# Batch-normalised pair products on one core: the head rebuilt, and the short rows' products moved

## The chip, the cores and the metric

One core of a Trainium2 chip runs the whole kernel. The metric is the device time of one execution in microseconds; the kernel before takes 1979.55 us (median of three runs, 1979.31 to 1979.63). The core has TensorE (PE, its weight loads shown as PEld), VectorE (DVE), ScalarE (ACT), GpSimd (POOL), and SyncE (SP), which here issues DMA transfers only. A q behind an engine's name (ACTq, SPq) stands for its instructions that issue transfers. PSUM is the memory that TensorE writes its results to, SBUF the working memory.

## The reference

All numbers are float32. `r_xi` and `r_xj` have shape 1024 x 39 x 16. For each pair of a row r and a smaller column c (741 pairs, the lower triangle of 39 x 39), the 16 x 16 outer product of a batch entry is normalised over the batch and its own 256 elements, scaled and shifted by the pair's gamma and beta, and multiplied by one 16 x 16 matrix W. The output is 1024 x 1 x 741 x 16 x 16, 777 MB.

```python
cross = xj[:, rows, :, None] * xi[:, cols, None, :]
mean = jnp.mean(cross, axis=(0, 2, 3), keepdims=True)
var = jnp.mean(jnp.square(cross - mean), axis=(0, 2, 3), keepdims=True)
normed = (cross - mean) * jax.lax.rsqrt(var + BN_EPS)
normed = normed * gamma[None, :, None, None] + beta[None, :, None, None]
out = normed[:, :, None, :, :] * W[None, None, :, :, :]
```

## The kernel before, in words

**Layout.** The batch is laid out as 128 partitions x 8 entries (`t`). The whole of xi and xj stays in SBUF. With the scale s and the shift t of a pair, an output element is (s xi xj + t) W.

**The head** (L66 to L240) finds s and t. The x arrays come in four pieces each, xj through SP's queue and xi through ACT's. Gamma and beta come as 38 one-row transfers each, gamma through SP (L83), beta through ACT (L84), into 39 x 39 squares. The first two batch entries give a shift for each field (row sums on VectorE, L109; a matmul of ones, L115; the shift written by ScalarE, L126). Then for each of four pieces and both arrays a deviation from the shift is made (L135, five on POOL and three on VectorE, three buffers), squared on ScalarE (L142), summed on VectorE (L144), and the mean's deviation is put beside it (L146). Gram matmuls (L158) sum over the batch. ScalarE copies the three results (L178), a chain of 39 x 39 operations on VectorE makes the variance and the reciprocal root (L191 to L215). To bring s and t of each pair to all partitions, VectorE spreads six rows at a time with a diagonal `eye` (L221), a matmul of ones copies them to 128 partitions (L228), and ScalarE copies each row out of PSUM into `st_sb` (L236).

**The body** makes the output in tiles of one row r and two batch entries; each row has four tiles, t0 = 0, 2, 4, 6. The order of tiles (L247 to L256) starts with row 19 and then pairs each long row r with the short row 38 - r: 20 with 18, 21 with 17, up to 37 with 1, and at last 38 alone. A long tile and its short partner together have 38 columns and fill one half of the buffer `y_sb`; the next two batch entries use the other half. For a tile, `scale_xi` (L267, POOL) multiplies xi by s into one of two `xs` buffers. `products` multiplies xs by each of the 16 elements of xj, for both batch entries: 24 operations on ScalarE (L292) and 8 on POOL (L294), each writing every 16th element of the tile, so that each waits until the stores of the old contents of the tile's whole place have landed. Where r is 6 or less (`VECTOR_ROW`), VectorE makes the products in two broadcast operations instead (L282). `finish` adds t and multiplies by W, one operation a column on VectorE (L319); for rows above 6, 13% of the columns are done by POOL (L305 and L309). It stores the tile in pieces of at most 14 columns through SP (L327), the POOL columns in the last piece.

**Order.** Each engine works through its instructions in program order. The code is written out by hand as a software pipeline (L332 on): in step k the products of tile k+1, the scaling for tile k+2, then the finishing of tile k; a short tile's products, made by VectorE, come behind the finishing of the tile ahead of it.

## Time and profile before

| what | value |
|---|---|
| median of three runs | 1979.55 us (1979.31 to 1979.63) |
| the profiled execution | 1979.6 us, span 1977.9 us |
| busy: DVE, ACT, POOL, PE | 1802.4, 1519.2, 1437.4, 18.6 us |
| written to HBM | 776.99 MB, 395 GB/s over the span |
| first store issued | 92.6 us |

The span reaches from the first to the last instruction; 1.7 us of the execution lie around it. The slices of the page cut the span into 40 equal parts of 49.4 us. Their digits are busy tenths, and the line DMA is the mean busy share of 16 DMA engines. In a table of stretches the DMA share reads 1.01 where the transfers have no gap.

### The profile page before, as it was taken

To read this page: it belongs to the slowest core of one execution; us is meant where nothing else is said; L and a number is where in the kernel's file an instruction comes from. 1 tells how busy PE (TensorE), PEld (TensorE's weight loads), DVE (VectorE), ACT (ScalarE), POOL (GpSimd) and SP (SyncE) were. 2 spreads that over 40 slices of the span, in tenths; PEclk is the share of its full clock that TensorE was granted. 3 is DMA by queue.
4 is the path that set the end of the run, shared out by engine and by line. 5 is a ranking of instruction groups with operands and counts; after the bars stand their busy time and mean duration, and the time that the engine had idled before them with its cause. 6 is when DMAs were issued, how large, how long until landed. Compare 5 with 4: busy or idle time off the path is not lost. (4 is left out here: it accounts for less than half of the span.)

```text
span 1977.9 us, 9219 instructions
## 1 busy us (share of the span) xinstructions
PE 18.6 (1%) x70; PEld 11.8 (1%) x70; DVE 1802.4 (91%) x2694; ACT 1519.2 (77%) x3127; POOL 1437.4 (73%) x1693
## 2 busy tenths in 40 slices
...
DMA  2199999999999999999999999999999999999998
GB/s 106 47 421 421 420 421 421 421 421 421 422 425 425 423 425 425 425 423 425 424 421 422 420 421 418 412 389 386 393 392 403 403 411 411 407 407 403 395 379 375
DMA packets 79760, 782.84 MB, mean 396 GB/s; under 512 B 4905, under 2 KB 5929, under 8 KB 14153
## 3 DMA queue, kind: packets, MB, share of 16 engines
...
q10 hardware_dynamic: 652, 2.56, 0.3%
...
q14 instruction: 72, 0.58, 0.1%
HBM read 5.25 MB, written 776.99 MB: 395 GB/s over the span
## 5 line engine op out<-in xcount | busy, mean ns | idle before, releaser
L319 DVE SCALAR_TENSOR_TENSOR y_sb<-y_sb,st_sb,w_dve 128x512 f32<-128x512 f32 x2588 | 1711.0, 742 | 133.5 <-issue 96.7
L292 ACT ACTIVATE y_sb<-xs,xj_sb 128x320 f32<-128x320 f32 (+21 forms) x3072 | 1500.8, 581 | 366.2 <-DMA out_dram<-y_sb 324.6
L294 POOL TENSOR_SCALAR y_sb<-xs,xj_sb 128x320 f32<-128x320 f32 (+22 forms) x1024 | 556.7, 566 | 188.9 <-DMA out_dram<-y_sb 155.3
L309 POOL TENSOR_TENSOR y_sb<-y_sb,w_sb 128x1024 f32<-128x1024 f32 (+4 forms) x128 | 431.2, 3369 | 10.7
L267 POOL TENSOR_TENSOR xs<-xi_sb,st_sb 128x608 f32<-128x608 f32 (+37 forms) x152 | 190.0, 1253 | 275.5 <-DVE y_sb L282 178.5
L305 POOL TENSOR_SCALAR y_sb<-y_sb,st_sb 128x512 f32<-128x512 f32 x376 | 253.8, 692 | 1.7 <-ACT y_sb L292 1.7
L282 DVE TENSOR_TENSOR y_sb<-xs,xj_sb 128x1536 f32<-128x1536 f32 (+5 forms) x48 | 50.1, 1085 | 0.0
L135 POOL TENSOR_TENSOR dev<-xj_sb,shift 128x1248 f32<-128x1248 f32 x4 | 9.3, 2325 | 36.4 <-ACT shift_r L129 28.8
L126 ACT ACT_TABLE_LOAD x1 | 1.3, 1283 | 29.8 <-DMA b_sq<-in_L_rec_beta_dram 29.8
L142 ACT ACTIVATE dev<-dev 128x1248 f32<-128x1248 f32 x8 | 9.9, 1243 | 14.7 <-POOL dev L135 11.5
L146 DVE SCALAR_TENSOR_TENSOR fa<-total,shift 128x78 f32<-128x78 f32 x4 | 3.1, 764 | 11.1 <-ACT shift_r L129 11.1
L109 DVE TENSOR_REDUCE total<-xj_sb 128x78 f32<-128x1248 f32 x4 | 5.8, 1454 | 8.0 <-DMA xj_sb<-in_r_xj_dram 8.0
L236 ACT COPY st_sb<-ps 128x38 f32<-128x38 f32 (+37 forms) x38 | 4.3, 219 | 8.7 <-PE ps L228 8.7
L228 PE MATMUL ps<-wide,ones 39*128 39x468 f32 (+1 forms) x14 | 10.2, 921 | 5.7 <-DVE wide L221 5.7
L221 DVE TENSOR_TENSOR wide<-stq,eye 39x468 f32<-39x468 f32 (+1 forms) x7 | 4.0, 593 | 3.7 <-PE ps L228 3.6
L144 DVE TENSOR_REDUCE fb<-dev 128x78 f32<-128x1248 f32 x4 | 5.7, 1442 | 1.4 <-ACT dev L142 1.4
L144 DVE TENSOR_REDUCE fa<-dev 128x78 f32<-128x1248 f32 x4 | 5.8, 1444 | 1.0 <-ACT dev L142 1.0
L158 PE MATMUL ps_g<-fb,fa 128*39 128x79 f32 x32 | 5.8, 338 | 41.4 <-DVE fb L144 41.4
L109 DVE TENSOR_REDUCE total<-xi_sb 128x78 f32<-128x1248 f32 x4 | 5.8, 1443 | 0.0
L135 DVE TENSOR_TENSOR dev<-xi_sb,shift 128x1248 f32<-128x1248 f32 x3 | 5.2, 1773 | 0.0
L146 DVE SCALAR_TENSOR_TENSOR fb<-total,shift 128x78 f32<-128x78 f32 x4 | 5.2, 1290 | 0.0
L158 PEld LDWEIGHTS ps_g<-fb,fa 128*39 128x39 f32 x32 | 4.3, 182 | 42.0 <-issue 30.9
...
## 6 DMA issues: line engine op xcount, KB each, us to landing
...
```

What stands on the lines that cost most here:

```text
L109: nc.vector.tensor_reduce(total[:, t0 : t0 + TS, x], src[:, t0 : t0 + TS], AX.X, ALU.add)
L135: engine.tensor_tensor(dev, src[:, t0 : t0 + TS], shift[:, x : x + 1, :].unsqueeze(3).to_broadcast([P, TS, F, E]), ALU.subtract,)
L144: nc.vector.tensor_reduce(to, dev, AX.X, ALU.add)
L158: nc.tensor.matmul(acc[0:F, 0 : 2 * F + 1], lhs, fb[:, t], start=t == 0, stop=t == NT - 1)
L228: nc.tensor.matmul(ps.rearrange("p r x f -> p (r x f)"), ones[0:F, :], wide.rearrange("p r f -> p (r f)"), start=True, stop=True,)
L267: nc.gpsimd.tensor_tensor(xs, xi_sb[:, t0 : t0 + T, 0:r, :], s_sb[:, :, n0 : n0 + r, :].to_broadcast([P, T, r, E]), ALU.mult,)
L282: nc.vector.tensor_tensor(y[:, t], xs[:, t].unsqueeze(2).to_broadcast([P, r, E, E]), xj_sb[:, t0 + t, r : r + 1, :].unsqueeze(3).to_broadc ...
L292: nc.scalar.activation(y[:, t, :, i, :], xs[:, t], AF.Copy, scale=scale)
L294: nc.gpsimd.tensor_scalar(y[:, t, :, i, :], xs[:, t], scale, 1.0, ALU.mult, ALU.mult)
L305: nc.gpsimd.tensor_scalar(y[:, :, c, :], y[:, :, c, :], t_sb[:, n0 + c : n0 + c + 1], 1.0, ALU.add, ALU.mult)
L309: nc.gpsimd.tensor_tensor(y[:, :, split:r, :], y[:, :, split:r, :], w_sb.unsqueeze(1).to_broadcast([P, T, r - split, EE]), ALU.mult,)
L319: nc.vector.scalar_tensor_tensor(y[:, :, c, :], y[:, :, c, :], t_sb[:, n0 + c : n0 + c + 1], w_dve.to_broadcast([P, T, EE]), ALU.add, ALU. ...
```

## The change

1. Gamma and beta are loaded by one broadcast each to all partitions (`gb_all`), beta still through ACT's queue. The 39 x 39 chain ends in the bare reciprocal root and in minus mean times root; gamma and beta are applied behind the spreading.
2. Rows are spread by one small matmul for each row, with a selector `pick[:, r, :]` (39 x 128, ones in partition r) as weights; POOL makes all 39 selectors in one operation on 4992 elements in a partition. Two VectorE operations a group bring the result through gamma and beta into `st_sb`. The first group is row 19 alone.
3. The four tiles of row 19 take the four quarters of `y_sb`. Scratch of the head lies in the third and fourth quarter: seven deviation buffers, and everything else with the selectors.
4. The products of the first two tiles are made from xi without s ("raw"), on ScalarE between the statistics' steps, and the last 12 of the second tile on POOL. When s and t are known, `affine` applies them in place, even columns on ScalarE, odd ones on POOL, and `weigh` multiplies by W on VectorE, several columns in one operation. The first tile is stored in pieces of 3, 6 and 10 columns.
5. All eight deviations are made by POOL. The fa/fb step reads the shift from PSUM (`ps_u`). The copy of W into PSUM is made early.
6. `VECTOR_ROW` is gone: rows 1 to 6 have their products made by ScalarE and POOL as all others, and rows 4 to 6 give POOL one column.

```diff
 BN_EPS = 1e-5
-VECTOR_ROW = 6
 PIECE = 14
+FIRST_PIECES = (0, 3, 9, 19)
-DEV_ON_VECTOR = ((2, 1), (4, 1), (6, 1))
-ROW_GROUPS = ((19, 25), (13, 19), (25, 31), (7, 13), (31, 37), (1, 7), (37, 39))
+ROW_GROUPS = ((19, 20), (15, 19), (20, 25), (25, 32), (1, 15), (32, 39))
...
-    ) as devp, tc.tile_pool(name="ps", bufs=1, space=bass.MemoryType.PSUM) as psp, tc.tile_pool(
...
-        for r in range(1, F):
-            n0 = first[r]
-            nc.sync.dma_start(g_sq[r : r + 1, 0:r], gamma[n0 : n0 + r].unsqueeze(0))
-            nc.scalar.dma_start(b_sq[r : r + 1, 0:r], beta[n0 : n0 + r].unsqueeze(0))
...
-        for r0, r1 in ROW_GROUPS:
-            n = r1 - r0
-            wide = devp.tile([F, n, 2 * F], F32, tag="wide", name="wide")
-            nc.vector.tensor_tensor(
-                wide,
-                stq.rearrange("p x f -> p (x f)").unsqueeze(1).to_broadcast([F, n, 2 * F]),
-                eye[:, r0:r1].unsqueeze(2).to_broadcast([F, n, 2 * F]),
-                ALU.mult,
-            )
...
-            for r in range(r0, r1):
-                nc.scalar.copy(st_sb[:, :, first[r] : first[r] + r], ps[:, r - r0, :, 0:r])
...
+    flat = y_sb.rearrange("p n e -> p (n e)")
+    place = {"dev": half * EE, "rest": (half + half // 2) * EE}
+    stop = {"dev": (half + half // 2) * EE, "rest": 2 * half * EE}
...
+    devs = [scratch("dev", P, T, F, E) for _ in range(7)]
+    ones = scratch("rest", P, P)
+    pick = scratch("rest", F, F, P)
+    gb_all = scratch("rest", P, 2, NP)
...
+    def raw_products(n, engine, steps):
+        r, t0, _ = tiles[n]
+        for step in steps:
+            t, i = divmod(step, E)
+            yield lambda t=t, i=i: product(n, engine, t, i, xi_sb[:, t0 + t, 0:r, :])
+    def emit(work, count):
+        for _, step in zip(range(count), work):
+            step()
...
-            if r <= VECTOR_ROW:
-                nc.vector.tensor_tensor(
-                    y[:, t],
-                    xs[:, t].unsqueeze(2).to_broadcast([P, r, E, E]),
-                    xj_sb[:, t0 + t, r : r + 1, :].unsqueeze(3).to_broadcast([P, r, E, E]),
-                    ALU.mult,
+            for i in range(E):
+                product(n, nc.scalar if i < E - POOL_I else nc.gpsimd, t, i, xs[:, t])
...
+    def affine(n):
+        r = tiles[n][0]
+        y = view(n)
+        for c in range(r):
+            s_c = st_sb[:, 0, first[r] + c : first[r] + c + 1]
+            t_c = t_sb[:, first[r] + c : first[r] + c + 1]
+            if c % 2 == 0:
+                nc.scalar.activation(y[:, :, c, :], y[:, :, c, :], AF.Identity, bias=t_c, scale=s_c)
+            else:
+                nc.gpsimd.tensor_scalar(
+                    y[:, :, c, :], y[:, :, c, :], s_c, t_c, ALU.mult, ALU.add
                 )
...
+    def weigh(n, bounds):
+        y = view(n)
+        for c0, c1 in zip(bounds, bounds[1:]):
+            nc.vector.tensor_tensor(
+                y[:, :, c0:c1, :],
+                y[:, :, c0:c1, :],
+                w_dve.unsqueeze(1).to_broadcast([P, T, c1 - c0, EE]),
+                ALU.mult,
+            )
+            store(n, c0, c1)
...
-        split = r - (int(r * POOL_SHARE + 0.5) if r > VECTOR_ROW else 0)
+        y = view(n)
+        split = r - int(r * POOL_SHARE + 0.5)
...
-        for k in range(len(tiles)):
-            if k + 1 < len(tiles) and tiles[k + 1][0] > VECTOR_ROW:
-                products(k + 1)
-            if k + 2 < len(tiles):
-                scale_xi(k + 2)
-            finish(k)
-            if k + 1 in xs_of:
-                products(k + 1)
+        nc.gpsimd.dma_start(w_sb[:, 0, :], w.rearrange("o i j -> (o i j)").partition_broadcast(P))
+        nc.sync.dma_start(gb_all[:, 0], gamma.partition_broadcast(P))
+        nc.scalar.dma_start(gb_all[:, 1], beta.partition_broadcast(P))
+        nc.gpsimd.memset(ones, 1.0)
+        nc.gpsimd.affine_select(
+            out=pick, in_=ones[0:F, :].unsqueeze(1).to_broadcast([F, F, P]),
+            compare_op=ALU.is_equal, fill=0.0, base=0,
+            pattern=[[-1, F], [0, P]], channel_multiplier=1,
+        )
...
+        def deviation(n):
+            t0, x = n // 2 * T, n % 2
+            nc.gpsimd.tensor_tensor(
+                devs[n % 7],
+                sources[x][:, t0 : t0 + T],
+                shift[:, x : x + 1, :].unsqueeze(3).to_broadcast([P, T, F, E]),
+                ALU.subtract,
+            )
...
+            stt(
+                to[:, t0 : t0 + T, 0:F],
+                total[:, t0 : t0 + T, part(x)],
+                1.0 / E,
+                ps_u[:, x : x + 1, :].to_broadcast([P, T, F]),
+                ALU.mult,
+                ALU.subtract,
+            )
...
+        raw0 = raw_products(0, nc.scalar, range(32))
+        raw1 = raw_products(1, nc.scalar, range(20))
+        sums(0)
+        emit(raw0, 8)
+        nc.scalar.copy(w_dve, w_sb)
...
+        ps_u = ps_s[:, 2 * F : 4 * F].rearrange("p (x f) -> p x f", x=2)
+        nc.scalar.copy(ps_u, shift)
+        sums(2)
+        for n in range(7):
+            deviation(n)
+        for n in range(2 * NT // T):
+            square(n)
+            emit(raw0, 3)
+            if n % 2 == 1 and n < 5:
+                sums(n + 3)
+            moments(n)
+            if n == 0:
+                deviation(7)
+            means(n)
+            if n % 2 == 1:
+                gram(n // 2 * T)
+        emit(raw_products(1, nc.gpsimd, range(20, 32)), 12)
+        emit(raw1, 6)
...
+        for to, acc in zip((g1, g2, g3), ps_g):
+            nc.scalar.activation(to, acc[0:F, 0 : 2 * F + 1], AF.Copy, scale=1.0 / NB)
...
+        emit(raw1, 6)
...
+        nc.vector.reciprocal(inv, var)
+        nc.scalar.activation(rstd, inv, AF.Sqrt)
+        emit(raw1, 8)
+        nc.vector.tensor_mul(inv, var, rstd)
+        nc.vector.tensor_mul(inv, inv, rstd)
+        nc.vector.tensor_scalar(inv, inv, -0.5, 1.5, ALU.mult, ALU.add)
+        nc.vector.tensor_mul(stq[:, 0], rstd, inv)
+        stt(stq[:, 1], mean, -1.0, stq[:, 0], ALU.mult, ALU.mult)
...
+        def spread(r0, r1):
+            n0, n1 = first[r0], first[r1 - 1] + r1 - 1
+            ps = psx.tile([P, 512], F32, tag="ps", name="ps")
+            ps_v = ps[:, 0 : 2 * (n1 - n0)].rearrange("p (x n) -> p x n", x=2)
+            for r in range(r0, r1):
+                nc.tensor.matmul(
+                    ps_v[:, :, first[r] - n0 : first[r] - n0 + r],
+                    pick[:, r, :],
+                    stq[:, :, 0:r],
+                    start=True,
+                    stop=True,
+                )
+            nc.vector.tensor_tensor(
+                st_sb[:, :, n0:n1],
+                ps_v,
+                gb_all[:, 0:1, n0:n1].to_broadcast([P, 2, n1 - n0]),
+                ALU.mult,
+            )
+            nc.vector.tensor_add(st_sb[:, 1, n0:n1], st_sb[:, 1, n0:n1], gb_all[:, 1, n0:n1])
+        spread(*ROW_GROUPS[0])
+        affine(0)
+        weigh(0, FIRST_PIECES)
+        scale_xi(2)
+        spread(*ROW_GROUPS[1])
+        spread(*ROW_GROUPS[2])
+        affine(1)
+        weigh(1, bounds(tiles[1][0]))
+        for group in ROW_GROUPS[3:]:
+            spread(*group)
+        for n in range(1, len(tiles)):
+            if n + 1 < len(tiles):
+                products(n + 1)
+            if n + 2 < len(tiles):
+                scale_xi(n + 2)
+            if n >= RAW:
+                finish(n)
```

The order on ScalarE in the head. Before, from the last load of beta to the first row copied to `st_sb` (shift is the shift, dev a deviation, g a Gram result, rstd the root):

```order
L84 DMA b_sq<-in_L_rec_beta_dram 1x38
L126 ACT_TABLE_LOAD
L126 ACTIVATE shift<-ps_s 128x78
L129 ACTIVATE shift_r<-ps_r 39x1
L142 ACTIVATE dev<-dev 128x1248 x8
L178 ACTIVATE g_256<-ps_g_175 39x79
L178 ACTIVATE g_257<-ps_g_176 39x79
L178 ACTIVATE g_258<-ps_g_177 39x79
L240 COPY w_dve<-w_sb 128x256
L208 ACT_TABLE_LOAD
L208 ACTIVATE rstd<-inv 39x39
L236 COPY st_sb<-ps 128x2x19
```

Nothing of the body stands ahead of the spreading. ScalarE now, from its first instruction to the first square; L130 are raw products, L316 to L321 the shift and its companions, L275 the squares:

```order
L235 DMA xi_sb<-in_r_xi_dram 128x1248 x4
L238 DMA y_sb<-in_L_rec_beta_dram 128x741
L130 ACT_TABLE_LOAD
L130 ACTIVATE y_sb<-xi_sb,xj_sb 128x19x16 x8
L306 COPY w_dve<-w_sb 128x256
L316 ACTIVATE y_sb<-ps_s 128x78
L319 ACTIVATE y_sb<-ps_r 39x1
L321 COPY ps_s<-y_sb 128x78
L275 ACTIVATE y_sb<-y_sb 128x1248
```

Eight products of the first tile have moved ahead of the shift. And further on ScalarE now, from the last square's products over the copies of the Gram results (L344) and the root (L368) to the affine step (L181) and the third tile's products:

```order
L130 ACTIVATE y_sb<-xi_sb,xj_sb 128x19x16 x9
L344 ACTIVATE y_sb<-ps_g_75 39x79
L344 ACTIVATE y_sb<-ps_g_76 39x79
L344 ACTIVATE y_sb<-ps_g_77 39x79
L130 ACTIVATE y_sb<-xi_sb,xj_sb 128x19x16 x6
L368 ACT_TABLE_LOAD
L368 ACTIVATE y_sb<-y_sb 39x39
L130 ACTIVATE y_sb<-xi_sb,xj_sb 128x19x16 x8
L181 ACTIVATE y_sb<-y_sb,st_sb 128x2x256 x20
L130 ACTIVATE y_sb<-xs_4_283,xj_sb 128x19x16 x24
```

The loads of beta are gone but for one, and the raw products stand between the statistics' steps: nine ahead of the copies, six ahead of the root and eight ahead of the affine step.

The order on VectorE in the long rows. Before, about the first tiles of row 32 with row 6 (L319 are columns, L282 the short row's products):

```order
L319 SCALAR_TENSOR_TENSOR y_sb<-y_sb,st_sb,w_dve 128x2x256 x1680
L282 TENSOR_TENSOR y_sb<-xs_0_5982,xj_sb 128x1536 x2
L319 SCALAR_TENSOR_TENSOR y_sb<-y_sb,st_sb,w_dve 128x2x256 x34
L282 TENSOR_TENSOR y_sb<-xs_2_6065,xj_sb 128x1536 x2
L319 SCALAR_TENSOR_TENSOR y_sb<-y_sb,st_sb,w_dve 128x2x256 x34
```

A tile pair's 34 columns are cut by two products. VectorE now, from the last group of the spreading on (L222 are columns):

```order
L390 TENSOR_TENSOR st_sb<-ps,y_sb 128x2x105
L396 TENSOR_TENSOR st_sb<-st_sb,y_sb 128x105
L390 TENSOR_TENSOR st_sb<-ps,y_sb 128x2x245
L396 TENSOR_TENSOR st_sb<-st_sb,y_sb 128x245
L222 SCALAR_TENSOR_TENSOR y_sb<-y_sb,st_sb,w_dve 128x2x256 x2310
```

The two-operation products in the middle of the columns are gone; the columns follow each other from the third tile to row 37.

The order on ScalarE about the same rows, row 31 to row 32. Before:

```order
L292 ACTIVATE y_sb<-xs_6_5870,xj_sb 128x7x16 x24
L292 ACTIVATE y_sb<-xs_0_5913,xj_sb 128x32x16 x24
L292 ACTIVATE y_sb<-xs_2_5993,xj_sb 128x32x16 x24
L292 ACTIVATE y_sb<-xs_4_6074,xj_sb 128x32x16 x24
L292 ACTIVATE y_sb<-xs_6_6155,xj_sb 128x32x16 x24
```

A short row with 7 columns has its 24 products here, one with 6 has none. And now:

```order
L130 ACTIVATE y_sb<-xs_6_5739,xj_sb 128x7x16 x24
L130 ACTIVATE y_sb<-xs_0_5782,xj_sb 128x32x16 x24
L130 ACTIVATE y_sb<-xs_0_5851,xj_sb 128x6x16 x24
L130 ACTIVATE y_sb<-xs_2_5894,xj_sb 128x32x16 x24
L130 ACTIVATE y_sb<-xs_2_5964,xj_sb 128x6x16 x24
```

The short row's 24 products stand between those of two long tiles.

314 lines of the change are left out of this document (132 added, 182 removed).

## The prediction

> **What bounds the kernel now.** I read the page's slices first, then the stretches late in the run, then the timeline of the head. The slices show two different kernels: two slices of 49 us almost without transfers, then transfers all the time, at 420 GB/s in the first half and less in the second.
>
> ```profile
> DMA  2199999999999999999999999999999999999998
> GB/s 106 47 421 421 420 421 421 421 421 421 422 425 425 423 425 425 425 423 425 424 421 422 420 421 418 412 389 386 393 392 403 403 411 411 407 407 403 395 379 375
> ```
>
> The output is nearly all the traffic (777 MB written), so the time is: the wait until stores start, plus 777 MB at the rate that is kept up. The table of stretches shows what the rate hangs on. Its columns are the stretch, busy time of PE, PEld, DVE, ACT and POOL, the granted clock, the DMA share and GB/s. The first row is an early stretch, the others run from row 32 of the triangle (1277 us) to row 37.
>
> ```profile
> 104.00:141.00 37.00, 0.00 (x0) 0.00 (x0) 37.00 (x57) 37.00 (x85) 31.67 (x43) 0.50 1.01 420
> 1277.00:1302.80 25.80, 0.00 (x0) 0.00 (x0) 25.77 (x37) 16.38 (x27) 16.91 (x19) 0.50 0.95 395
> 1302.80:1406.30 103.50, 0.00 (x0) 0.00 (x0) 103.36 (x146) 63.19 (x103) 61.44 (x63) 0.50 0.93 386
> 1406.30:1507.60 101.30, 0.00 (x0) 0.00 (x0) 101.16 (x146) 60.60 (x96) 60.32 (x61) 0.50 0.95 397
> 1507.60:1606.00 98.40, 0.00 (x0) 0.00 (x0) 98.26 (x144) 59.52 (x93) 62.42 (x60) 0.50 0.96 402
> 1606.00:1704.00 98.00, 0.00 (x0) 0.00 (x0) 94.64 (x142) 65.13 (x99) 67.42 (x63) 0.50 0.99 411
> 1704.00:1803.00 99.00, 0.00 (x0) 0.00 (x0) 92.06 (x142) 66.12 (x98) 68.97 (x65) 0.50 0.97 404
> 1803.00:1872.00 69.00, 0.00 (x0) 0.00 (x0) 62.22 (x97) 43.58 (x64) 40.82 (x39) 0.50 0.97 405
> ```
>
> At a share of 1.01 the transfers are full and 420 GB/s is their ceiling. The late rows have shares of 0.93 to 0.99, and the rate goes down with the share (386/0.93 is 415, 420/1.01 is 416): DMA has gaps there, it is not slower. From 1277 to 1606 DVE has no pause at all. One column of a tile is 2 x 128 x 1024 B = 0.262 MB, 0.624 us of DMA; a long row with its short partner has 38 columns, 23.7 us.
>
> The head, from the timeline (start, duration, engine, line, operation, count, in brackets idle time before and its releaser):
>
> ```profile
> 0.81 2.26 ACTq L69 DMA_DIRECT2D xi_sb<-in_r_xi_dram  x4
> 2.35 0.22 POOL L88 TENSOR_SCALAR_AFFINE_SELECT eye<-ones 39x39 f32<-39x39 f32 x1
> 7.38 22.36 ACTq L84 DMA_DIRECT2D b_sq<-in_L_rec_beta_dram  x38
> 29.77 1.28 ACT L126 ACT_TABLE_LOAD   x1 [29.77 <-DMA b_sq<-in_L_rec_beta_dram]
> 31.33 0.24 DVE L146 SCALAR_TENSOR_TENSOR fa<-total,shift 128x78 f32<-128x78 f32 x1 [11.08 <-ACT shift_r L129]
> 31.38 2.36 POOL L135 TENSOR_TENSOR dev<-xj_sb,shift 128x1248 f32<-128x1248 f32 x1 [28.82 <-ACT shift_r L129]
> 31.49 2.35 DVE L146 SCALAR_TENSOR_TENSOR fb<-total,shift 128x78 f32<-128x78 f32 x1
> 44.14 2.56 ACT L142 ACTIVATE dev<-dev 128x1248 f32<-128x1248 f32 x2 [4.57 <-POOL dev L135]
> 56.04 1.45 DVE L144 TENSOR_REDUCE fb<-dev 128x78 f32<-128x1248 f32 x1 [1.37 <-ACT dev L142]
> 58.86 0.76 ACT L178 ACTIVATE g<-ps_g 39x79 f32<-39x79 f32 x3 [2.85 <-PE ps_g L158]
> 59.38 0.25 DVE L197 SCALAR_TENSOR_TENSOR q<-g,shift_r,g 39x39 f32<-39x39 f32 x1 [1.89 <-ACT g L178]
> 61.99 0.39 DVE L207 RECIPROCAL inv<-var 39x39 f32<-39x39 f32 x1
> 62.69 0.19 DVE L209 TENSOR_TENSOR inv<-var,rstd 39x39 f32<-39x39 f32 x1 [0.30 <-ACT rstd L208]
> 64.02 0.19 DVE L215 TENSOR_TENSOR stq<-b_sq,mean 39x39 f32<-39x39 f32 x1
> 65.01 10.24 PE L228 MATMUL ps<-wide,ones 39*128 39x468 f32 x14 [5.67 <-DVE wide L221]
> 75.44 3.97 POOL L294 TENSOR_SCALAR y_sb<-xs,xj_sb 128x304 f32<-128x304 f32 x8 [6.74 <-PE ps L228]
> 75.67 34.78 ACT L292 ACTIVATE y_sb<-xs,xj_sb 128x304 f32<-128x304 f32 x79
> 86.39 23.79 DVE L319 SCALAR_TENSOR_TENSOR y_sb<-y_sb,st_sb,w_dve 128x512 f32<-128x512 f32 x36 [14.43 <-ACT y_sb L292]
> 92.60 16.71 SPq L327 DMA_DIRECT2D out_dram<-y_sb  x4
> ```
>
> ACT issues 38 one-row loads of beta until 29.8 and only then loads its table and writes the shift for which POOL and DVE wait. The statistics end at 64.2, the rows are spread until 75.7, and the first products and columns bring the first store at 92.6.
>
> **The head, step by step.** Prices: a 304-element ACT product 34.78/79 = 0.44 us, a POOL product 3.97/8 = 0.50, a DVE column 23.79/36 = 0.661, a deviation on POOL 2.36, a square 2.56/2 = 1.28. The rest is in these groups (busy and mean of one; then idle time):
>
> ```profile
> L292 ACT ACTIVATE y_sb<-xs,xj_sb 128x512 f32<-128x512 f32 x96 | 59.2, 707 | 29.7 <-DMA out_dram<-y_sb 11.4 <-POOL y_sb L309 9.4 <-DVE y_sb L319 8.8
> L292 ACT ACTIVATE y_sb<-xs,xj_sb 128x112 f32<-128x112 f32 x96 | 27.1, 375 | 0.0
> L282 DVE TENSOR_TENSOR y_sb<-xs,xj_sb 128x1536 f32<-128x1536 f32 x8 | 13.7, 1752 | 0.0
> L305 POOL TENSOR_SCALAR y_sb<-y_sb,st_sb 128x512 f32<-128x512 f32 x376 | 253.8, 692 | 1.7 <-ACT y_sb L292 1.7
> L309 POOL TENSOR_TENSOR y_sb<-y_sb,w_sb 128x512 f32<-128x512 f32 x20 | 25.4, 1271 | 1.7
> L294 POOL TENSOR_SCALAR y_sb<-xs,xj_sb 128x112 f32<-128x112 f32 x32 | 10.8, 358 | 0.0
> ```
>
> *To the shift.* The 38 beta loads become one broadcast. It is still issued by ACT behind the first xi load, so at 7.4 as now, for 22.36/38 = 0.6 us. Then table load 1.28, eight raw products 3.5, the copy of w (priced as a product, 0.44), and the shift at 13.5; ACT is free of its two companions at 13.8. Now the shift is there at 31.3, so 18 us go. The gamma and beta broadcasts carry 0.76 MB, 1.8 us of DMA, behind the x loads; their data is needed only at 46, which hides them. On POOL stands the new selector, 4992 elements in a partition. The trace has only the 39-element one, 0.22 us. Its cost lies between that of a plain POOL pass (L305 takes 0.69 us for 512 elements, so 6.7) and 0.22/39 x 4992 = 28 us, if all of the 0.22 were per element. It has from 2.4 to 13.5 to hide in, 11 us. I take the lower end, because L305 is as long an operation of the same engine as the trace has with one input, and count nothing; the upper end is a rival.
>
> *To the last square.* Eight deviations back to back on POOL end at 13.5 + 8 x 2.36 = 32.4. ACT does a square and three raw products for each, 1.28 + 1.32 = 2.6, from 15.9 on: the eighth square ends at 15.9 + 7 x 2.6 + 1.28 = 35.4, so ACT paces this stage. Now the last reduction waits until 56.04. The seven scratch buffers in place of three take away the waits for buffers, and DVE's three deviations go to POOL.
>
> The fa/fb step takes 0.24 us on DVE alone but 2.35 beside a POOL deviation; the change reads the shift from PSUM there. The Trainium skill (SBUF — State Buffer, section Who interferes with whom) says that a DVE instruction with two SBUF inputs waits for a running GpSimd instruction that reads SBUF, and the trace agrees, 2.35 against 0.24. By that rule the additions of beta in the second and third spread, which have two SBUF inputs, could each wait for one POOL column of 0.69 us: the sum below would be 1.4 us longer.
>
> *To the first store.* Last reduction and mean 1.7, Gram products 1.4 (57.5 to 58.86): 38.5. ACT has nine raw products behind the last square and comes free at 39.4, so it sets the three copies out of PSUM. DVE starts 0.5 later (39.9) and reaches the reciprocal's end 3.0 later, 42.9, as from 59.38 to 62.38 now. ACT's six raw products and the table load of the square root end at 44.1, and the root waits 1.2 us for them. Five DVE operations of 0.22: 45.4. One 38-wide selector matmul in place of 468-wide ones: the old 14 took 10.24, 0.73 each; with start and end I take 0.9, between 0.2 and 2.0: 46.3, and two DVE operations 0.5, 46.9. But ACT still has eight raw products, until 44.3 + 3.5 = 47.8, and so sets the affine step. Its 512-element pass is 59.2/96 = 0.617; three columns, two on ACT and one on POOL beside it, are done at 49.1. DVE multiplies them by w in one operation, 1536 elements, 1.75: 50.8. The first store is issued at 50.9 instead of 92.6, 41.7 earlier. The products of this tile, 10.7 us on the path now (75.67 to 86.39), lie in ACT's waits of the statistics; where those waits are over they show, as the 0.9 and 1.2 us here and the 0.9 before the affine step.
>
> *Until DMA is full.* DVE then paces, at 1.75/3 = 0.58 a column: 6 columns at 54.4, 10 at 60.2, two spreads 1.2, 9 at 66.7, 10 at 72.5, three spreads 2.7, and nine columns of the third tile (0.661 each) at 81.1. In these 30.2 us DMA sends 38 columns, 23.7 us: it idles 6.5. After that DVE needs 17 x 0.661 = 11.2 for a 19-column tile against 11.9 of DMA, and ACT 24 x 0.44 = 10.6, so it stays full. Products of the fourth tile must wait for the last spreads, since the selectors lie where it is written; ACT comes free of the third tile at about 71 and the spreads end at 75.2, and DVE wants that tile at 86, so this is hidden.
>
> Head: 41.7 - 6.5 = **-35.2 us**.
>
> **The short rows.** Where r is 32 or more, its partner's products are now two DVE operations in the middle of DVE's columns. The first two lines are the chain of waits at row 32, the other three the timeline at rows 36 and 37:
>
> ```profile
> 1310.61 3.35 DVE y_sb L282 x2
> 1336.45 3.35 DVE y_sb L282 x2
> 1723.82 16.09 ACT L292 ACTIVATE y_sb<-xs,xj_sb 128x576 f32<-128x576 f32 x24 [8.58 <-DMA out_dram<-y_sb]
> 1740.00 20.50 DVE L319 SCALAR_TENSOR_TENSOR y_sb<-y_sb,st_sb,w_dve 128x512 f32<-128x512 f32 x31 [1.53 <-issue]
> 1773.23 16.41 ACT L292 ACTIVATE y_sb<-xs,xj_sb 128x592 f32<-128x592 f32 x24 [9.19 <-DMA out_dram<-y_sb]
> ```
>
> A pair takes 25.8 us in row 32, and DVE is what fills it: 34 columns, 22.5, and 3.35 for the products. The change moves the products to 24 ACT and 8 POOL operations, and one column of rows 6, 5 and 4 to POOL. DVE is left with 33 columns, 21.8, under DMA's 23.7. ACT gets 24 x 0.28 = 6.8 at most (the 112-element group; shorter rows cost less) beside 24 x 0.617 = 14.8: 21.6. POOL, 61.44/103.5 of the time busy now, 15.3 a pair, gets 8 x 0.36 + 0.69 + 1.27 = 4.8: 20.1. All three lie under 23.7, and then DMA bounds.
>
> In rows 36 and 37 something else bounds already: DVE stands idle 1.5 us and starts at 1740.0, when ACT's products have ended (1723.82 + 16.09), and ACT had waited 8.6 us for a store out of its half of y_sb, the next time 9.2. From 1723.82 to 1773.23 one half turns once in 49.4 us: 24 products, the columns, the last piece's store. Two pairs of DMA are 47.4. Nothing that the change moves lies in this turn, since ACT's 9 us of waiting hold the short products. A row that is shorter by one column takes about 1 us off the turn (24 x 0.013 for the products, from the two ACT groups, and 0.66 on DVE or DMA), so 34 is at 47.4, the border, and 32 and 33 are under it. I take 23.7, 23.8 and 24.1 a pair for rows 32 to 34 and leave 35 to 38 as they are. From 1277 to 1606 there are 13 pairs, four of each and one of row 35: 94.8 + 95.2 + 96.4 + 24.6 = 311, against 329. Late rows: **-18 us**. All of it at 420 GB/s (129.9 MB in those four stretches) would be 309, -20.
>
> Sum against the profiled execution, 1979.6 us with a span of 1977.9 and as good as the median of 1979.55: 1979.6 - 35.2 - 18 = **1926** us.
>
> **The rivals.**
>
> *The slot turn goes too.* If DVE's short products also delay rows 35 to 37, all from 1277 to 1872 runs at 420 GB/s: 108.2 MB from 1606 to 1872 would take 258 instead of 266, and rows 32 to 34 gain their last 2: 1916 us. For it: DVE is 93% busy there. Against it: DVE waits for ACT there, and ACT for the store.
>
> *The selector is late.* At 28 us it ends at 30.6, the deviations at 49.5, the last square at 50.8 instead of 35.4: 15.4 us, 1942 us.
>
> *Short pieces are simply slower.* If the rate falls in the late rows because pieces of 1 to 6 columns move slower, only the head gains: 1944 us. For it: the rate is at its lowest where short pieces appear. Against it: the DMA share falls with it. The Trainium skill (SBUF — State Buffer, section Summary: rules for kernel authors) would have one plan with about 358 GB/s between HBM and SBUF. By that all late rows are already above the ceiling, and the same 1944 us would follow; the trace shows 420 for a thousand microseconds, and the measurement decides.
>
> *Slower.* The short products enter the turn: ACT does them in order, and they wait for the partner's store of two pairs ago. If that store lands so late that the next long row's products wait behind them, a turn grows from 49.4 by up to 6.8, to 56.2. Rows 32 to 37 have 12 turns, 595 us now: 674, so 1979.6 - 35.2 + 79 = 2023 us. It eats the head's gain from 2.9 us a turn on. For it: the order on ACT allows no overtaking. Against it: the short store is issued straight behind the long row's last piece, and at ACT's first product of the next pair 8 to 9 us of waiting have gone by.
>
> **How the numbers follow.** The forecast gets 0.74; the turn that goes too 0.07, the late selector 0.07, the slower pieces 0.07, the slower case 0.03; 0.02 stays for what I did not see. About 0.2% is what a measurement of this kernel can tell from no change, 4 us. All cases but the slower one gain far more: faster 0.95, same 0.01, slower 0.04. The forecast's own range is 1920 to 1939: the first store between 46 and 57 (matmul, selector's and affine step's bounds), late rows between 12 and 20. With the cases at 1916 and 1942 the range is 1914 to 1942.
>
> **What would show it.** Right: the shift on ACT at 13 to 14 us, the last square at 35, the first store at 48 to 54, DMA gaps of 5 to 8 us until 81; rows 32 and 33 at a DMA share of 1.00 with DVE no longer without pause, rows 35 to 38 as before. Wrong: a POOL selector beyond 13 us; DVE's multiplications by w above 0.66 a column, which would leave DMA idle in the first tiles; ACT waiting for short stores ahead of long products; a late rate still under 410 GB/s in row 32.

## The result and the profile after

The changed kernel takes 1929.09 us (median of 4 runs, 1928.77 to 1929.3) against 1979.54 for the kernel before; the ratio is 0.9745, with a 95% interval from 0.9728 to 0.9762. The profiled execution of the changed kernel has a span of 1927.5 us, 50.4 shorter than before. The slices of its page (what the transfers moved), to be held against those of before:

```profile
GB/s 125 326 421 421 420 421 421 421 421 421 424 426 423 424 425 423 426 423 426 423 421 421 421 421 416 411 420 416 414 415 414 415 414 415 405 406 402 393 389 373
```

Transfers begin a slice earlier (326 GB/s in the second slice in place of 47), and the low in the middle of the second half, 386 to 393 GB/s before, is now 414 to 420. The last five slices are nearly as they were, 373 to 406 against 375 to 407.

The head, from the timeline (start, duration, engine, line, operation, count, in brackets the idle time before and its releaser):

```profile
2.35 4.63 POOL L242 TENSOR_SCALAR_AFFINE_SELECT y_sb<-y_sb 39x4992 f32<-39x4992 f32 x1
7.45 0.34 ACTq L238 DMA_DIRECT2D y_sb<-in_L_rec_beta_dram  x1
12.94 0.22 ACT L316 ACTIVATE y_sb<-ps_s 128x78 f32<-128x78 f32 x1
32.76 1.23 ACT L275 ACTIVATE y_sb<-y_sb 128x1248 f32<-128x1248 f32 x1
37.84 0.45 ACT L344 ACTIVATE y_sb<-ps_g 39x79 f32<-39x79 f32 x3
42.50 0.19 DVE L370 TENSOR_TENSOR y_sb<-y_sb 39x39 f32<-39x39 f32 x1 [1.59 <-ACT y_sb L368]
45.88 14.20 ACT L181 ACTIVATE y_sb<-y_sb,st_sb 128x512 f32<-128x512 f32 x20
49.27 49.50 SPq L168 DMA_DIRECT2D out_dram<-y_sb  x9
58.86 0.99 DVE L396 TENSOR_TENSOR st_sb<-st_sb,y_sb 128x66 f32<-128x66 f32 x1
60.17 0.28 DVE L396 TENSOR_TENSOR st_sb<-st_sb,y_sb 128x110 f32<-128x110 f32 x1
74.55 0.67 DVE L390 TENSOR_TENSOR st_sb<-ps,y_sb 128x490 f32<-128x490 f32 x1 [2.37 <-PE ps L383]
75.87 24.44 DVE L222 SCALAR_TENSOR_TENSOR y_sb<-y_sb,st_sb,w_dve 128x512 f32<-128x512 f32 x37
```

One beta load stands where 38 stood, the shift (L316) is written at 12.94 us in place of 31.06, the last square ends at 33.99, and the first store is issued at 49.27 in place of 92.60. From 75.87 to 141 VectorE makes ordinary columns without a pause. The table of stretches of the changed kernel (columns as in the prediction: busy time of PE, PEld, DVE, ACT, POOL, the granted clock, DMA share, GB/s); the lines from 1207 on hold about four pairs of tiles each, the last pair of one row and three of the next, from row 31 to row 37; the last one holds row 37's last pair, row 38 and the end:

```profile
47.00:80.00 33.00, 13.62 (x62) 13.12 (x61) 29.44 (x22) 30.32 (x59) 23.80 (x36) 1.00 0.74 303
80.00:95.00 15.00, 0.00 (x0) 0.00 (x0) 15.00 (x24) 15.00 (x35) 14.83 (x21) 1.00 0.82 341
95.00:141.00 46.00, 0.00 (x0) 0.00 (x0) 46.00 (x71) 46.00 (x106) 43.88 (x58) 1.00 1.01 421
1207.00:1304.00 97.00, 0.00 (x0) 0.00 (x0) 87.27 (x133) 85.82 (x195) 77.88 (x101) 1.00 1.00 415
1304.00:1400.00 96.00, 0.00 (x0) 0.00 (x0) 87.56 (x133) 85.32 (x194) 78.10 (x101) 1.00 1.00 415
1400.00:1496.00 96.00, 0.00 (x0) 0.00 (x0) 87.12 (x133) 84.88 (x193) 77.50 (x101) 1.00 0.99 415
1496.00:1592.00 96.00, 0.00 (x0) 0.00 (x0) 87.09 (x132) 84.69 (x191) 76.95 (x97) 1.00 0.99 414
1592.00:1688.00 96.00, 0.00 (x0) 0.00 (x0) 87.26 (x132) 84.72 (x193) 76.96 (x96) 1.00 0.98 410
1688.00:1788.00 100.00, 0.00 (x0) 0.00 (x0) 87.26 (x132) 85.03 (x193) 76.95 (x96) 1.00 0.97 405
1788.00:1927.00 139.00, 0.00 (x0) 0.00 (x0) 109.07 (x165) 72.07 (x121) 77.65 (x66) 1.00 0.92 385
```

Where the time came from. By 141 us the kernel before had written 20.0 MB (12 us at 373 GB/s from the first store on, 37 us at 420), this one 10.0 + 5.1 + 19.4 = 34.5 MB: 14.5 MB, 34.4 us at 421 GB/s. That lead stays nearly as it is until row 32. In the four stretches from 1207 to 1592 VectorE is busy 90 to 91% of the time, not 100, and the share is 0.99 to 1.00: the stretch of before from 1277 to 1606, 329 us at 395 GB/s on average, is 329 x 395/415 = 313 us at the new rate, 16 us less. 34.4 + 16 is the 50.4 of the spans.

The same can be read from VectorE's columns alone. These are its groups at the start of row 32 (the first two lines) and of row 35, each time in the kernel before (L319) and then in the changed one (L222). The third line begins with four columns of a short row (2.6 us), so row 35 starts at 1570.0 there:

```profile
1266.24 18.52 DVE L319 SCALAR_TENSOR_TENSOR y_sb<-y_sb,st_sb,w_dve 128x512 f32<-128x512 f32 x28 [1.87 <-issue]
1232.38 21.81 DVE L222 SCALAR_TENSOR_TENSOR y_sb<-y_sb,st_sb,w_dve 128x512 f32<-128x512 f32 x33 [2.80 <-issue]
1567.36 22.47 DVE L319 SCALAR_TENSOR_TENSOR y_sb<-y_sb,st_sb,w_dve 128x512 f32<-128x512 f32 x34
1519.83 21.81 DVE L222 SCALAR_TENSOR_TENSOR y_sb<-y_sb,st_sb,w_dve 128x512 f32<-128x512 f32 x33 [2.18 <-issue]
```

The changed kernel is 33.9 us ahead when row 32 starts and 50.2 when row 35 starts; rows 32 to 34 take 287.4 us in place of 303.8. From there on the lead stays: 50.3, 49.8 and 50.6 us at the starts of rows 36, 37 and 38, 50.4 at the end.

### The profile page after: what moved, and what is told of

It is laid out like the page before. It is cut to its first block, busy times and chain, and to the rows that moved or that the text cites. A ratio compares the mean times of both kernels' runs of the same rounds, so it can differ in the third digit from the quotient of the medians.

```text
span 1927.5 us, 10086 instructions
## 1 busy us (share of the span) xinstructions
PE 25.5 (1%) x132; PEld 23.8 (1%) x132; DVE 1732.3 (90%) x2603; ACT 1663.4 (86%) x3690; POOL 1528.2 (79%) x1918
## 5 line engine op out<-in xcount | busy, mean ns | idle before, releaser
L222 DVE SCALAR_TENSOR_TENSOR y_sb<-y_sb,st_sb,w_dve 128x512 f32<-128x512 f32 x2542 | 1679.7, 742 | 158.5 <-issue 147.1
L130 ACT ACTIVATE y_sb<-xs,xj_sb 128x256 f32<-128x256 f32 (+33 forms) x3600 | 1613.4, 542 | 218.7 <-DMA out_dram<-y_sb 166.2
L132 POOL TENSOR_SCALAR y_sb<-xs,xj_sb 128x256 f32<-128x256 f32 (+33 forms) x1200 | 604.3, 527 | 198.5 <-DMA out_dram<-y_sb 131.3
L150 POOL TENSOR_TENSOR xs<-xi_sb,st_sb 128x576 f32<-128x576 f32 (+37 forms) x150 | 188.0, 1253 | 146.4 <-ACT y_sb L130 146.4
L210 POOL TENSOR_SCALAR y_sb<-y_sb,st_sb 128x512 f32<-128x512 f32 x384 | 259.6, 693 | 1.7 <-ACT y_sb L130 1.7
L130 ACT ACTIVATE y_sb<-xi_sb,xj_sb 128x304 f32<-128x304 f32 x52 | 23.9, 533 | 0.0
L191 DVE TENSOR_TENSOR y_sb<-y_sb,w_dve 128x5120 f32<-128x5120 f32 (+3 forms) x5 | 20.9, 4205 | 3.2 <-ACT y_sb L181 3.2
L183 POOL TENSOR_SCALAR y_sb<-y_sb,st_sb 128x512 f32<-128x512 f32 x18 | 13.5, 772 | 7.5 <-DVE st_sb L396 7.5
L383 PE MATMUL ps<-y_sb 39*128 39x38 f32 (+37 forms) x76 | 16.9, 398 | 20.1 <-DVE st_sb L390 13.9
L383 PEld LDWEIGHTS ps<-y_sb 39*128 39x128 f32 x76 | 16.4, 328 | 20.7 <-DVE st_sb L390 14.2
L181 ACT ACTIVATE y_sb<-y_sb,st_sb 128x512 f32<-128x512 f32 x20 | 14.2, 798 | 0.0
L275 ACT ACTIVATE y_sb<-y_sb 128x1248 f32<-128x1248 f32 x8 | 9.8, 1228 | 2.2 <-POOL y_sb L266 2.2
L132 POOL TENSOR_SCALAR y_sb<-xi_sb,xj_sb 128x304 f32<-128x304 f32 x12 | 5.9, 509 | 0.0
## 6 DMA issues: line engine op xcount, KB each, us to landing
out_dram<-y_sb SPq DMA_DIRECT2D x23, 2304.0 KB, 15.6
```

Source lines behind the costliest of these rows:

```text
L130: nc.scalar.activation(y, src, AF.Copy, scale=scale)
L132: engine.tensor_scalar(y, src, scale, 1.0, ALU.mult, ALU.mult)
L150: nc.gpsimd.tensor_tensor(xs, xi_sb[:, t0 : t0 + T, 0:r, :], s_sb[:, :, n0 : n0 + r, :].to_broadcast([P, T, r, E]), ALU.mult,)
L181: nc.scalar.activation(y[:, :, c, :], y[:, :, c, :], AF.Identity, bias=t_c, scale=s_c)
L183: nc.gpsimd.tensor_scalar(y[:, :, c, :], y[:, :, c, :], s_c, t_c, ALU.mult, ALU.add)
L191: nc.vector.tensor_tensor(y[:, :, c0:c1, :], y[:, :, c0:c1, :], w_dve.unsqueeze(1).to_broadcast([P, T, c1 - c0, EE]), ALU.mult,)
```

## The experiments

All times are to be held against 1929.1 us for the changed kernel and 1979.6 for the kernel before.

### The late rows

**VectorE makes the short rows' products again, in the changed kernel.**

```diff
+VECTOR_ROW = 6
 def products(n):
+            if r <= VECTOR_ROW:
+                nc.vector.tensor_tensor(...)
+                continue
-        split = r - int(r * POOL_SHARE + 0.5)
+        split = r - (int(r * POOL_SHARE + 0.5) if r > VECTOR_ROW else 0)
```

> The changed kernel, with the products of rows 1 to 6 made on VectorE again and no GpSimd share of these rows, as in the kernel before; the head stays as changed. Theory (the later part of the gain is VectorE's relief in rows 32 to 36): 16 us come back, about 1945 us, and rows 32 to 34 take 25.8 us a pair of tiles in place of 24.0; VectorE has no pause there. Rival (the later gain comes from the head, whose changed order lets the stores run on without a break): 1929 us, and the rows keep their 24.0.

1946.11 us, 17.0 more. The diff leaves out the order of the calls, in which a short row's products come behind the columns ahead of them, as in the kernel before. The stretch of the late rows in its trace:

```profile
1277.00:1600.00 323.00, 0.00 (x0) 0.00 (x0) 322.23 (x464) 194.91 (x305) 202.31 (x198) 1.00 0.95 397
```

VectorE is busy 322.23 of 323 us and the share is back at 0.95. Rows 32 to 34 take 303.8 us again, by the starts of VectorE's columns. The theory holds.

**The other half of it: the kernel before, with the short rows off VectorE.**

```diff
-VECTOR_ROW = 6
+VECTOR_ROW = 0
```

> The kernel before, with only the constant for the rows whose products VectorE makes set from 6 to 0; its head stays. Theory (head and later part add, without touching each other): 1979.5 less 16 to 18, about 1963 us, and rows 35 and 36 gain about 0.5 us a pair, as between the two kernels. Rival (the later gain needs the new head): 1979 us.

1964.11 us, 15.5 less than before. Over the same 329 us as before it reaches the changed kernel's rate:

```profile
1277.00:1606.00 329.00, 0.00 (x0) 0.00 (x0) 297.96 (x451) 292.49 (x661) 264.57 (x343) 0.50 1.00 415
```

Rows 32 to 34 take 288.1 us. That rows 35 and 36 would gain half a microsecond a pair did not come: they take 96.2 and 99.0 us, against 96.2 and 97.9 before. So the two halves of the change add: the head is worth 33.5 us (before, to the run with VectorE's products) to 35.0 (this run, to the changed kernel), the late rows 15.5 to 17.0.

**Is it VectorE's own time, or that others waited for its products?**

```diff
             store(n, c0, c1)
+        if r >= 32:
+            for _ in range(F - 1 - r):
+                nc.vector.tensor_tensor(ps_r..., w_sb..., w_dve..., ALU.mult)
```

> The changed kernel, with useless work put on VectorE behind each long tile of row r from 32 on: 38 - r multiplications of 128x512 into a PSUM tile that nobody reads any more, at about 0.6 us each (3.6 us a pair in row 32, 0.6 in row 37). It puts VectorE's load of before back, without making GpSimd's scaling of a slice wait for VectorE's products (178.5 us of waits in the kernel before). Theory (VectorE's own time paced rows 32 to 35): about 1943 us, with rows 32 to 34 at about 25.7 us a pair. Rival (what the old rows lost was GpSimd's wait for the short products, which held up the scaled slices and so ScalarE): 1929 us, VectorE's pauses only get shorter.

1944.74 us. No other engine reads what the added operations write; the group of them and a stretch in rows 32 and 33:

```profile
L233 DVE TENSOR_TENSOR ps_r<-w_sb,w_dve 128x512 f32<-128x512 f32 x84 | 58.2, 693 | 2.1
```

```profile
1304.00:1400.00 96.00, 0.00 (x0) 0.00 (x0) 95.42 (x146) 78.48 (x183) 76.17 (x95) 1.00 0.93 388
```

They cost 0.69 us each, 58 us in all, and 15.6 us of that shows at the end; the rest lies in pauses that VectorE has beside the transfers. VectorE's time alone brings back 15.6 of the 17.0 us; GpSimd's wait for the short products (178.5 us in the kernel before) is not needed for that loss. Whether the remaining 1.4 us come from it was not tried.

### The head

**The 38 loads on ScalarE's queue.**

```diff
         nc.scalar.dma_start(gb_all[:, 1], beta.partition_broadcast(P))
+        for r in range(1, F):
+            nc.scalar.dma_start(b_sq[r : r + 1, 0:r], beta[first[r] : first[r] + r].unsqueeze(0))
```

> The changed kernel, with the 38 one-row loads of beta put back on ScalarE's queue (into a scratch tile that nobody reads) ahead of its first work: 38 issues at 0.59 us, some 22 us. Theory (the path through shift, deviations, squares, gram matrix and root has no slack behind the loads): shift at about 34.5 in place of 12.9, and the whole rest 21 to 22 us later, 1950.5 us. Rival (part of the path's slack, VectorE's or GpSimd's, absorbs it, or the end of the head is set elsewhere): under 1945 us.

1951.2 us, 22.1 more. From its timeline, where L319 is the write of the shift:

```profile
11.89 17.58 ACTq L241 DMA_DIRECT2D y_sb<-in_L_rec_beta_dram  x38
34.62 0.22 ACT L319 ACTIVATE y_sb<-ps_s 128x78 f32<-128x78 f32 x1
70.97 21.92 SPq L169 DMA_DIRECT2D out_dram<-y_sb  x5
```

The shift is 21.7 us later, the first store 21.7, the end 22.1: the path from the shift to the stores has no slack that would hide a microsecond of issue. The price of 0.59 us an issue is an average over pauses. In the kernel before the first three issues come at 7.38, 11.53 and 14.60 and take 0.23 to 0.48 us, and the last 14 take 4.90 us, 0.35 each. Here 3.9 us pass between the one beta load (until 8.00) and the first of the 38. What the queue waits for in these pauses, the traces don't show.

**Without the raw products.** The first two tiles go the ordinary way after the statistics.

```diff
-    RAW = 2
+    RAW = 0
-        emit(raw0, 8)
-            emit(raw0, 3)
-        emit(raw_products(1, nc.gpsimd, range(20, 32)), 12)
...
-        affine(0)
-        weigh(0, FIRST_PIECES)
-        scale_xi(2)
+        scale_xi(0)
+        products(0)
+        scale_xi(1)
```

> The changed kernel without the raw products: the first two tiles go the ordinary way after the statistics (slice scaled, 24 + 8 products, column operations on VectorE, pieces of 9 and 10); the statistics, selector matmuls and broadcast loads stay as changed. First store: scaling and spread done at about 46.5, products 10.6, nine columns at 0.66: about 63 us in place of 49.3. Theory (continuous transfers decide): the changed kernel's transfers are worth a continuous start at 81.8 - 23.7 = 58.1 us, so 4 to 6 us more, about 1934 us. Rival (the first store decides): 14 us more, 1943 us.

1934.87 us, 5.8 more. In its timeline the copies out of PSUM (L338) come at 33.99, 3.9 us before those of the changed kernel, since no products stand between the squares; the first store comes 13.8 us later:

```profile
33.99 0.76 ACT L338 ACTIVATE y_sb<-ps_g 39x79 f32<-39x79 f32 x3 [3.02 <-PE ps_g L298]
63.10 33.87 SPq L168 DMA_DIRECT2D out_dram<-y_sb  x7
```

Of 13.8 us of later first store 8 are not felt. The raw products bring 13.8 of the 43.3 us by which the changed kernel's first store is earlier, and 5.8 of its time.

**The first tile in one store.**

```diff
 def weigh(n, bounds):
-            store(n, c0, c1)
+            if n > 0:
+                store(n, c0, c1)
+        if n == 0:
+            store(n, 0, bounds[-1])
```

> The changed kernel, with one store for all 19 columns of the first tile in place of three; everything else keeps its place, so the first byte leaves at about 58.7 us of the span in place of 49.3. Theory (what counts is when the transfers become continuous, which the third tile's columns set at about 82 us; by then 38 columns, 23.7 us, have to be out, so a start at 58.6 is still in time): 1929 us, at most 0.5 more. Rival (every microsecond of the first store's time is a microsecond of the end): 9.4 more, 1938.5 us.

1929.03 us, the same, with the first store 8.9 us later. The timeline of SP and two stretches:

```profile
58.19 40.21 SPq L168 DMA_DIRECT2D out_dram<-y_sb  x7
```

```profile
47.00:80.00 33.00, 13.16 (x60) 12.66 (x59) 29.90 (x22) 30.24 (x59) 23.73 (x36) 1.00 0.64 270
80.00:95.00 15.00, 0.00 (x0) 0.00 (x0) 15.00 (x24) 15.00 (x35) 14.83 (x21) 1.00 1.01 420
```

Up to 95 us it has written 8.9 + 6.3 = 15.2 MB, the changed kernel 15.1. The pieces of 3, 6 and 10 columns buy nothing: what they send early is idle time later, before the third tile's first piece.

**The shift read from SBUF.**

```diff
-        nc.scalar.copy(ps_u, shift)
...
-                ps_u[:, x : x + 1, :].to_broadcast([P, T, F]),
+                shift[:, x : x + 1, :].to_broadcast([P, T, F]),
```

> The changed kernel, with the eight small subtractions of the means reading the shift from SBUF and not from a copy in PSUM, so that both of their inputs lie in SBUF while GpSimd makes deviations. In the kernel before three such operations took 2.35 us in place of 0.23. Theory (VectorE is full from 16.9 to 35.6 us and each subtraction that falls beside a deviation waits for that deviation's end, five or six of them, 1 to 2 us each): 5 to 11 us more, about 1936 us. Rival (the operations are off the path, ScalarE's squares pace it): 1929 us.

1930.73 us, 1.6 more: nearer to the rival than to the theory. From the timelines of VectorE and GpSimd:

```profile
18.04 1.97 DVE L286 SCALAR_TENSOR_TENSOR y_sb<-y_sb 128x78 f32<-128x78 f32 x1
32.68 0.22 DVE L286 SCALAR_TENSOR_TENSOR y_sb<-y_sb 128x78 f32<-128x78 f32 x1
```

```profile
17.60 2.32 POOL L266 TENSOR_TENSOR y_sb<-xj_sb,y_sb 128x1248 f32<-128x1248 f32 x1
```

The operation of 0.22 us that starts beside a deviation ends within 0.1 us of that deviation's end (18.04 + 1.97 = 20.01 beside 17.60 + 2.32 = 19.92); at 32.68 GpSimd is through with its deviations and it takes 0.22. The mechanism is there, and only the size was wrong: four of eight were caught and lost 3.1 us together; the other four came after GpSimd's last deviation, which ends at 31.3. From there to 37.3 GpSimd makes raw products of 0.50 us each (L132); the three operations that start beside these take 0.22 to 0.23 and do not wait. The copies out of PSUM come 1.0 us later than in the changed kernel, since in the changed kernel VectorE has a pause of 0.85 us in this stage that takes up part of the loss. The addition of 0.99 us at 58.86 in the changed kernel ends beside GpSimd's affine step (59.66) and may be of the same kind.

**A third PSUM tile for the spreads.**

```diff
-    psx = ctx.enter_context(tc.tile_pool(name="psx", bufs=2, ...))
+    psx = ctx.enter_context(tc.tile_pool(name="psx", bufs=3, ...))
-    w_dve = psp.tile([P, 1, EE], F32, name="w_dve")
+    w_dve = ps_s[:, 256:512].unsqueeze(1)
```

> The changed kernel, with three PSUM tiles in place of two for the spreads (the weights' copy in PSUM shares the bank of the sums to make room). VectorE then need not wait 2.4 us at 72 us of the span for the selector matmuls of the last group, and the third tile's columns begin at about 73.5 in place of 75.9. Theory (these columns set the start of continuous transfers): 2 to 2.4 us less, 1926.8 us. Rival (the tiles behind them are held by ScalarE's products or GpSimd's): 1929 us.

1926.19 us, 2.9 less. In this run the copy of W into PSUM stands behind the shift as well, and the first store comes 0.3 us earlier (49.00). The third tile's columns begin 3.0 us earlier, and the first pause of the transfers behind 80 us is gone:

```profile
72.86 27.73 DVE L222 SCALAR_TENSOR_TENSOR y_sb<-y_sb,st_sb,ps_s 128x512 f32<-128x512 f32 x42
```

```profile
80.00:95.00 15.00, 0.00 (x0) 0.00 (x0) 15.00 (x24) 15.00 (x35) 14.92 (x24) 1.00 1.01 419
```

Together with the one-store run: 8.9 us at the first store are worth nothing, 3.0 us at the third tile's columns are worth 2.9.

### The last rows

**Row 38 with a tile's columns ahead of the next products.**

```diff
+            last_row = tiles[n][0] == F - 1
+            if last_row:
+                finish(n)
             if n + 1 < len(tiles):
                 products(n + 1)
...
-            if n >= RAW:
+            if n >= RAW and not last_row:
                 finish(n)
```

> The changed kernel, with one order turned on GpSimd and ScalarE in row 38 alone (the last): a tile's own columns are finished before the next tile's products are issued. Theory (row 38 takes 27.0 us a tile because GpSimd goes round in a ring: its products 6.0, the scaled slice 2.2, its columns 3.4 and 5.6, then the store of 9.5 that frees the place): the products leave the ring, and the row falls to the slot turn's 24.7 or so, which is 6 to 7 us less, about 1922.5 us. Rival (the store itself and ScalarE's products pace the row): 1929 us; or slower, if the products that come later hold up VectorE.

1926.68 us, 2.4 less: a third of what the theory said. ScalarE's products of row 38, of the changed kernel and then of this one:

```profile
1821.50 16.73 ACT L130 ACTIVATE y_sb<-xs,xj_sb 128x608 f32<-128x608 f32 x24 [7.91 <-DMA out_dram<-y_sb]
1848.50 16.73 ACT L130 ACTIVATE y_sb<-xs,xj_sb 128x608 f32<-128x608 f32 x24 [10.28 <-DMA out_dram<-y_sb]
1875.42 16.73 ACT L130 ACTIVATE y_sb<-xs,xj_sb 128x608 f32<-128x608 f32 x24 [10.19 <-DMA out_dram<-y_sb]
```

```profile
1821.34 16.73 ACT L130 ACTIVATE y_sb<-xs,xj_sb 128x608 f32<-128x608 f32 x24 [7.78 <-DMA out_dram<-y_sb]
1847.89 16.72 ACT L130 ACTIVATE y_sb<-xs,xj_sb 128x608 f32<-128x608 f32 x24 [9.83 <-DMA out_dram<-y_sb]
1872.92 16.73 ACT L130 ACTIVATE y_sb<-xs,xj_sb 128x608 f32<-128x608 f32 x24 [8.30 <-DMA out_dram<-y_sb]
```

The distances fall from 27.0 and 26.9 to 26.6 and 25.0, and ScalarE still waits 8 to 10 us for a store. In the changed kernel the last store of a tile of row 38 waits for GpSimd's columns: it goes out at 1838.86 and 1865.86, 3.4 and 5.7 us after VectorE's last column. With the turned order it goes out right behind VectorE, at 1835.53 and 1860.03. So the ring on GpSimd is gone, and the transfers stand right behind it: a tile's place comes free 26.1 and 26.6 us after its first store (1821.79 to 1847.89, 1846.29 to 1872.92), and the transfers of a whole tile are 23.7 of these.

**A short last piece in rows 36 to 38.**

```diff
     def bounds(r):
+        if r >= 36:
+            return (0, 13, 26, r - 4, r)
```

> The changed kernel, with tiles of rows 36 to 38 stored in pieces of 13, 13, 6 to 8 and 4 columns in place of three of 12 or 13. Theory (rows 36 to 38 are paced by the turn of a half of the buffer: products, columns, store of the last piece, the next products; the last piece has 8 or 9 columns less, 5 to 6 us of transfer off a turn of 49 to 50 us for two tiles): rows 36 and 37 fall to the transfers' 24.0 a pair, row 38 from 27 to about 24 or 25, and the end of the span loses some 5 us of the last store: 8 to 11 us less, about 1920 us. Rival (the transfers themselves are slower there, 405 GB/s and less): 1929 us, or slower for a fourth store per tile.

1932.92 us, 3.8 more: the forecast falls. Two stretches, from row 35's last pair to row 37's third:

```profile
1592.00:1688.00 96.00, 0.00 (x0) 0.00 (x0) 87.20 (x132) 83.81 (x191) 76.86 (x96) 1.00 0.97 402
1688.00:1788.00 100.00, 0.00 (x0) 0.00 (x0) 86.82 (x132) 83.35 (x191) 76.92 (x96) 1.00 0.96 397
```

410 and 405 GB/s are now 402 and 397. But the edit does less than was expected of it. GpSimd makes the last five columns of these tiles, so with a last piece of four columns one of GpSimd's columns lies in the piece before it, and the two go out together. In row 38's first tile this is when GpSimd is through, and in row 37 when VectorE is:

```profile
1836.33 5.60 POOL L216 TENSOR_TENSOR y_sb<-y_sb,w_sb 128x2560 f32<-128x2560 f32 x1
1841.96 1.69 SPq L168 DMA_DIRECT2D out_dram<-y_sb  x2
```

So 12 columns are sent behind that wait in row 38, where the changed kernel sends 13, and 10 and 11 in rows 36 and 37 in place of 12 and 13. ScalarE's products of the next tile in that place start at 1852.60, 12.7 us after VectorE's last column (1818.13 + 21.81 = 1839.94), against 13.0 in the changed kernel. Whether a last piece that is really short would help, this run doesn't show. What it made longer is the first piece, 13 columns in place of 12. VectorE makes a column in 0.66 us and a transfer takes 0.62, so the whole tile's 23.7 us of transfer can begin when the first piece is ready. As an estimate, 0.66 us in each of six turns (12 tiles, two in a turn) is 4.0 us, near the 3.8; that the fourth store itself costs time is the other reading of this run.

**These three edits at once.** The third PSUM tile, row 38's turned order and the short last piece.

> The changed kernel with three edits at once: row 38's columns ahead of the next products on GpSimd and ScalarE (1926.7 us alone), the short last piece in rows 36 to 38, and the third PSUM tile for the spreads. Theory (they work in different places, the first two only partly): the sum of the three, 10 to 14 us less than the changed kernel, about 1917 us. Rival (the short piece takes away the ring that the turned order removes, and that order then only delays the next products): not under the short piece alone less 2.4 us, about 1918 to 1921 us.

1927.5 us. The three single effects, -2.9, -2.4 and +3.8, sum to 1927.6: they add, and the short piece is a loss here too. Both forecasts, 1917 us and 1918 to 1921, had counted it as a gain and missed.

**Four pieces of equal length in rows 37 and 38**, with the third PSUM tile and row 38's turned order:

```diff
     def bounds(r):
-        pieces = -(-r // PIECE)
+        pieces = -(-r // PIECE) + (r >= 37)
```

> The changed kernel with the third PSUM tile for the spreads and row 38's turned order (by their own runs 2.9 and 2.4 us less, together 1923.8), and rows 37 and 38 stored in four pieces of 9 or 10 columns in place of three of 12 or 13. Theory, formed on the run with the short last piece (a half of the buffer turns once in products 16.7, the first piece's columns, the whole tile's transfer of 23.7 and 2 for landing; VectorE makes a column in 0.66 and a transfer takes 0.62, so the first piece's length is what counts, not the last's): the first piece is 3 columns shorter and the pause behind it goes, 2 to 3 us off a turn of two tiles, against 0.3 for one more store: rows 37 and 38 are 4 to 6 us faster, about 1919 us. Rival (one more store costs 0.3 us a tile and nothing is won, as with the short last piece): 1926 us.

1917.01 us, ratio 0.9684 with an interval from 0.9671 to 0.9697 against the kernel before: 12.1 us faster than the changed kernel, and 6.8 faster than the other two edits by their own runs. ScalarE's products in row 38 and the stretches of rows 37 and 38:

```profile
1815.52 16.73 ACT L130 ACTIVATE y_sb<-xs,xj_sb 128x608 f32<-128x608 f32 x24 [7.38 <-DMA out_dram<-y_sb]
1840.46 16.73 ACT L130 ACTIVATE y_sb<-xs,xj_sb 128x608 f32<-128x608 f32 x24 [8.21 <-DMA out_dram<-y_sb]
1865.22 16.73 ACT L130 ACTIVATE y_sb<-xs,xj_sb 128x608 f32<-128x608 f32 x24 [8.03 <-DMA out_dram<-y_sb]
```

```profile
1681.00:1778.00 97.00, 0.00 (x0) 0.00 (x0) 86.53 (x132) 83.81 (x192) 76.42 (x94) 1.00 1.00 416
1778.00:1915.00 137.00, 0.00 (x0) 0.00 (x0) 112.85 (x171) 77.03 (x128) 79.18 (x72) 1.00 0.97 403
```

The distances are 24.9 and 24.8. Row 37, most of which lies in the first stretch, takes 97.1 us in place of 99.3 in the changed kernel, and row 38 with the end 107.1 in place of 111.4 with the turned order alone. In these two rows it has as many stores as the run with the short last piece, which lost: it is the lengths that differ. The first store of a tile now comes 6.2 us after VectorE's first column, not 8.1, and the place comes free 26.1 and 26.7 us after the first store, as with the turned order alone (26.1 and 26.6). That speaks for the first piece's length: three columns, 2.0 us, in each of four turns would be 7.9 us as an estimate, 6.8 came. The last piece became shorter too, 10 columns in place of 13, and since VectorE and the transfers go at nearly one pace, these numbers alone don't part the two; the first piece was not tried by itself.

## Why the prediction was right, point by point

**The head.** 34.4 us measured, 35.2 forecast. Each step came about where it was put, mostly 1 to 2 us earlier: the shift at 12.94 (13.5), the last square's end at 33.99 (35.4; a step of ScalarE took 2.45, not 2.6), the reciprocal's end at 40.91 (42.9), the affine step's start at 45.88 (47.8), the first store at 49.27 (50.9). ScalarE paces the squares as said, and the root's pause on VectorE is 1.59 us with the table load in it. The affine step's price was too low, 14.20/20 = 0.71 against 0.617.

The term that was mis-sized is the idle time between first store and full transfers: 6.5 us forecast, with 5 to 8 as the sign of being right, about 8.8 measured (75.87 + 9 x 0.661 = 81.8 for the third tile's first piece, 32.5 us behind the first store, less 23.7). The steps from the first store on went slower than summed: ScalarE's affine columns held VectorE back for 0.53 us, an addition of beta took 0.99, and the wait of 2.37 us for the last selector matmuls, which had no third PSUM tile to run ahead into, was not in the sum. So part of the earlier first store was given back there; the one-store run and the third PSUM tile show that only the later end of that stretch counts. The prediction's form, 41.7 less 6.5, was right because it charged the idle time.

**The selector.** 4.63 us, under the lower end of 6.7 to 28, and ready at 6.98, 6 us ahead of the shift. The rival of the late selector is out.

**The wait on VectorE beside GpSimd.** The Trainium skill (SBUF — State Buffer, section Who interferes with whom) has a VectorE instruction with two SBUF inputs wait for a running GpSimd instruction that reads SBUF. The first of the two additions of beta in question took 0.99 us (0.23 in the run without raw products) and the second 0.28, so one of the two was held up, by 0.8 us, and the sum is not 1.4 us longer. The run with the shift from SBUF agrees with the page beside the deviations, where four operations waited; beside GpSimd's products three of them did not wait, and the measurement decides there. It also shows that the changed place of the shift saves 1.6 us.

**The late rows.** 16 us measured, 18 forecast. VectorE's time was the cause, as the three runs show. By the starts of VectorE's columns, the thirteen pairs of the sum (four of each of rows 32 to 34 and the first of row 35) take 311.4 us in the changed kernel; 311 was forecast. Some of that is luck: the pairs take 23.9, 24.1 and 23.9 us in rows 32 to 34 and 24.0 in row 35, in place of 23.7, 23.8, 24.1 and 24.6, so the transfers' pace was taken too fast and the pace of rows 34 and 35 too slow, and the two errors cancel. The term that was mis-sized is the time before. 329 us were read between 1277 and 1606, edges that lie inside tiles (row 32 starts at 1266.24); the same thirteen pairs took 327.3 us.

The transfers run at 414 to 415 GB/s in these rows, where 420 was taken, at a share of 0.99 to 1.00 in place of 1.01. The rate for a share of one is the same within the rounding of the share (421/1.01 = 417, 415/1.00 = 415), so the rival of slower pieces is not borne out; what takes the last hundredth of the share stays open. The Trainium skill's 358 GB/s (SBUF — State Buffer, section Summary: rules for kernel authors) bounds nothing here: 415 GB/s are kept up in the very rows for which that rule would have left no gain.

Rows 35 to 38 were to stay as they are, and they do: 96.2, 97.9, 100.1 and 113.7 us before (row 38 with the end), 96.1, 98.4, 99.3 and 113.8 now. VectorE's load does not matter in row 35: with its short products back the row takes 95.7 us, with the idle work 96.4.

**The buffer's turn.** That something else than VectorE paces rows 36 to 38 was right, and so the rival in which all late rows reach 420 GB/s did not come. What the turn is made of was right only in part: the prediction named the products, the columns and the last piece's store. In row 38 the last store was held up by GpSimd's columns, which the turned order shows, 2.4 us in all. With GpSimd out of the way a place came free 26 us after the tile's first store, so the first piece's columns and the whole tile's transfer fit what the runs show better than the last piece's store alone; four equal pieces, with a shorter first one, gain 6.8 us. The slower rival, in which the short products enter the turn, did not come: ScalarE still waits ahead of the long rows' products for stores or VectorE's columns (1.9 to 4.3 us in rows 36 and 37, 7.4 to 9.2 before), and the run with the old kernel and the short rows off VectorE gains its 15.5 us with no loss behind.
